# Four-layer graph network on one NeuronCore: own rows added later, mask conversions spread over a stage, buffers and stores of two projections rearranged

## The chip, the cores and the metric

The kernel runs on one core of a Trainium2 chip. A core has a TensorE (PE) for matrix products, a VectorE (DVE), a ScalarE (ACT) and a GpSimd (POOL) for elementwise work, and a SyncE (SP) that only issues transfers; PE, DVE, ACT and POOL each execute their own instructions in order, and semaphores make one engine wait for another. Transfers (DMA) are issued from the queues of SP, ACT and POOL. The metric is the device time of one execution in microseconds, less being better. Matrix products read from on-chip buffers and leave their sums in PSUM, from where DVE or ACT takes them.

## The reference, cut to what matters

The input x has 2708 rows of 512 numbers, adj is a 2708 x 2708 matrix of 0 and 1. Four layers follow one another, each as x = layernorm(x + layer(x)):

```python
# layer 0: mean over the first 64 neighbours of each row, and the row itself
keep = Ab & (cumsum(Ab, axis=1) <= 64)
xj = leaky_relu((keep @ X) / max(cnt, 1) @ W_nb.T + b_nb)
out0 = leaky_relu(X @ W_line.T + b_line) + where(cnt > 0, xj, 0)
# layer 1: mean over all neighbours
self_f = x @ W_self + b_self
nb_f = (mask @ x / max(deg, 1)) @ W_nb + b_nb
out1 = relu(concat([self_f, nb_f]) @ W_comb + b_comb)
# layer 2: attention over the neighbours with 8 heads of 64 columns
# layer 3: attention with 8 heads, elu, attention with one head of 512 columns, elu, then
out3 = relu(h @ lin1_w + lin1_b) @ lin2_w + lin2_b      # 512 -> 1024 -> 512
```

## The kernel before, in words

The 2708 rows are worked on as NT = 22 tiles of P = 128 rows; the last tile has 20 rows. The whole mask stays on the chip, turned, in an 8-bit buffer maskT (one slab of 2816 columns for each tile). Rows of a layer's result go to DRAM and are fetched again where they are needed (fetched(), lines 162 to 165, issued by SP into a buffer called "rows" of the pool "ahead", which has three of them). A tile framework orders each engine's instructions and inserts the waits; `tc.issue_after(x)` puts an instruction behind another on its engine, and `pe` (lines 95 to 101) chains PE's instructions in the order written. Generators (todo, both) hand out small pieces of other work between the products of a loop.

Layer 0's products (loop from line 297 on). For each tile: the product with W_nb (product(), lines 226 to 229, four matmuls of 128x512), split into a high part on ACT and a low part yL on DVE (line 223); for 14 of the mask's tiles also a count on ACT (line 246) and the keep rule on DVE, in two halves, each a running sum (line 252) and a multiplication (line 255), and the turning of the mask by PE; then the product with W_line, the bias (line 317), leaky (line 186) and the addition of the tile's own rows x (line 319). The result u goes to r0_dram. The pair of lines 317 to 319 stands between the two halves of the keep rule on DVE. b_line is fetched on ACT's queue by bias() (lines 214 to 217).

Layer 0's aggregation (loop from line 450 on). Tiles are taken in blocks of four, with sums in PSUM; for each of 22 slabs ACT converts a piece of the mask (kT, line 335) and PE multiplies it with the high and the low part (line 460). Between these products come: the remaining masks (other_masks), the weights of layer 1 (weights1: W_self, W_nb and both halves of W_comb are fetched on SP's queue, some of them through "rows"), the attention vectors (vectors), and finish() for the block before (lines 376 to 386): it fetches r0, adds b_nb, applies leaky, adds r0, normalises, and stores x1. b_nb is another bias(), fetched when this stage begins, into the same single buffer as b_line.

Layer 1's first stage (loop from line 481 on). For each tile: product with W_nb (split as above), the conversion of one slab of the mask from a sign to 0 and 1 on DVE (line 485, 128x2816 eight-bit numbers), then the product with W_self, whose result goes to z1_dram. Its second stage (loop from line 495 on) multiplies the converted mask with the split rows (line 506); ACT widens eight slabs at a time (line 503).

Projections p2, p3 and p4 (project(), from line 566). For each tile: source() gives the rows, PE turns them, multiplies with the weights (line 627), and DVE and ACT make from the product the scaled rows R2 (line 656), and the columns ucol, ecol and vcol. keep_v() (lines 597 to 608) turns the last of them by PE, applies exp on ACT (line 605), collects the columns of a whole block of tiles in vrow, and stores each block at its end on SP's queue. In p3 source is summed() (lines 929 to 938): it fetches o of the attention before (into "rows") and x2 (into "spare", two buffers), multiplies (line 934), adds (line 935), normalises in place with the last step on ACT (line 118), and stores the rows as x3; the same buffer is then turned by PE. p4 takes its rows from elu_turned() and has no summed().

Attention (lines 703, 730, 895 and 799) and the last attention (line 1056) follow. The tiles' MLP is mlp() (lines 1007 to 1039): products with lin1 (line 1022), relu on ACT (line 1024), then for each tile eight products with lin2 (line 1031), the sum with x3, normalisation and the store to out. For the last pair, tiles 20 (128 rows) and 21 (20 rows), nothing else is left to run beside it.

A second, general program (from line 1106 on) is kept for inputs whose values leave the range that the first assumes; it isn't executed in these runs, and the change doesn't touch it.

Of the kernel before, what the change touches and what calls it, by code (L numbers as in the profile page):

```python
# [30 lines left out]
def kernel(  # L31
# [57 lines left out]

    o_dram = dram.tile([N, D], F32, name="o_dram")  # L90
    oT_dram, rc_dram = [], []

    behind = []

# [90 lines left out]
    def leaky(dst, u):  # L185
        return nc.vector.scalar_tensor_tensor(dst, u, 0.01, u, op0=OP.mult, op1=OP.max)
# [7 lines left out]
    with ExitStack() as phase:  # L194
# [16 lines left out]
        sums = lambda dtype=F32, shape=(P, D): ps_a.tile(list(shape), dtype, name="acc", tag="acc")  # L211
        sm = phase.enter_context(tc.tile_pool(name="l01", bufs=2))

        def bias(src):
            b = sm.tile([P, D], F32, name="bias", bufs=1)
            nc.scalar.dma_start(b, src)
            return b

        highs = {}
# [4 lines left out]

        def product(xT, n, w, which, order=as_it_comes):
            pm = ps_mm.tile([P, D], F32, name=f"pm{which}")
            for k in range(KD):
                order(nc.tensor.matmul(pm[:n], xT[:, k, :n], w[:, k, :], start=(k == 0), stop=(k == KD - 1)))  # L228
            return pm
# [45 lines left out]
        with ExitStack() as ph:  # L275
# [21 lines left out]
            for t in range(NT):  # L297
                n = rows(t)
                if t > 1:
                    lows[t] = keep_y(t, n, product(xTs(t, order=pe), n, wnT, 0, pe))  # L300
                xT = xTs(t)
                if t + 1 < NT:
                    xTs(t + 1, order=pe)
                while turned < counted - (t + 1 < NT):
                    for _ in turn(turned, masks(turned), lambda: sums(BF16, (P, G, P)), pe):
                        pass
                    turned += 1
                now = counted < min(HERE, -(-(t - 1) * HERE // (NT - 5)))
                if now:
                    m, places = masks(counted), st.tile([P, N // 2], BF16, name="places", bufs=1)  # L310
                    with tc.issue_after(highs[t].ins):
                        count(counted, m)
                    with tc.issue_after(lows[t].ins):
                        place(counted, m, places, 0, 2)
                pm = product(xT, n, wlT, 1, pe)
                u = sm.tile([P, D], F32, name="u")
                nc.vector.tensor_add(u[:n], pm[:n], b_line[:n])  # L317
                leaky(u[:n], u[:n])
                low = nc.vector.tensor_add(u[:n], u[:n], xs(t))
# [7 lines left out]

        with ExitStack() as ph:
            st = ph.enter_context(tc.tile_pool(name="l0b", bufs=1))
            b_nb = bias(bcast(l0_b_nb, D))  # L330

            def kept(b, j):
                w = (b[1] - b[0]) * P
# [42 lines left out]
            def finish(ts_, us):  # L376
                for t in ts_:
                    n, u = rows(t), us[t]
                    r0 = fetched(r0_dram, t, n)
                    nc.vector.tensor_add(u[:n], u[:n], b_nb[:n])  # L380
                    leaky(u[:n], u[:n])
                    yield
                    nc.vector.scalar_tensor_tensor(u[:n], u[:n], has[:n, t:t + 1], r0, op0=OP.mult, op1=OP.add)
# [156 lines left out]
        nc.vector.tensor_reduce(pick_c[:, g], rows_c, AX.X, OP.add)  # L540


    LAST, TWIN, few = NT - 1, 32, rows(NT - 1)
    assert few <= TWIN
# [21 lines left out]
    def project(name, source, layer, v_dram, cuts, turned=None, first=None):  # L566
# [12 lines left out]
        with ExitStack() as ph:  # L579
# [7 lines left out]
            width = max(z - a for a, z in cuts) * P  # L587
# [7 lines left out]
            vrows, bs, scaled = {}, {}, {}  # L595
# [344 lines left out]
    loads, ready = [], {}  # L940

# [30 lines left out]
    class Last:  # L972
# [34 lines left out]
        def mlp(self, t0, t1, h):  # L1007
# [11 lines left out]
            for f in range(KF):  # L1019
# [4 lines left out]
                nc.scalar.activation(gT[:, f, :w], pl[:, :w], AF.Relu, bias=self.b1[:, f:f + 1])  # L1024
                if f % 2:
                    yield
            for t in range(t0, t1):
                n = rows(t)
                pl = self.ps_l.tile([P, 512], F32, name="pl")
                for f in range(KF):  # L1030
                    nc.tensor.matmul(pl[:n], gT[:, f, (t - t0) * P:(t - t0) * P + n], self.lin2[:, f, :],  # L1031
                                     start=(f == 0), stop=(f == KF - 1))
                    if f == KF // 2 - 1:
                        yield
                y = (self.pool or sm).tile([P, D], F32, name="xT")
                nc.vector.tensor_add(y[:n], pl[:n], x3s[t])
                layer_norm(sm, y[:n], n, y[:n])
                (nc.sync if t1 == NT else nc.gpsimd).dma_start(out[t * P:t * P + n, :], y[:n])
                yield

    quads = [(t, min(t + 4, NT)) for t in range(0, NT, 4)]
# [385 lines left out]
```

## Time and profile before

| what | us |
|---|---|
| median of 3 runs | 2994.57 (2991.03 to 2997.17) |
| profiled execution | 2990.11 |
| its span | 2988.3 |
| PE busy | 2887.4 (97%) |
| DVE busy | 1997.9 (67%) |
| ACT busy | 1533.7 (51%) |
| POOL busy | 219.8 (7%) |

Stages of the profiled execution, by the start of their first matmul or last step, in us from the span's start:

| stage | from | to |
|---|---|---|
| layer 0: products | 0 | 221 |
| layer 0: aggregation, with the weights of layer 1 | 221 | about 500 |
| layer 1: products, then aggregation | about 500, 665 | 885 |
| p2, attention of layer 2 | 886, 977 | 1528 |
| p3, attention of layer 3 | 1528, 1640 | 2190 |
| p4, last attention and MLP | 2190, 2268 | 2988 |

The page gives busy times by engine and groups of equal instructions. A group's line reads: source line, engine, operation, out<-in by the program's names, shapes, the count; then busy time and the mean of one in ns; then the idle time of the engine just before and what ended it. A timeline line reads: start, length, engine, line, operation, and in brackets the idle time before it with the releaser. Since an engine executes in order, a long wait on one engine is only worth its length if the engine that sets the stage's end stands too.

### The profile page before, as it was taken

To read this page: it belongs to the slowest core of one execution; us is meant where nothing else is said; L and a number is where in the kernel's file an instruction comes from. 1 tells how busy PE (TensorE), PEld (TensorE's weight loads), DVE (VectorE), ACT (ScalarE), POOL (GpSimd) and SP (SyncE) were. 2 spreads that over 40 slices of the span, in tenths; PEclk is the share of its full clock that TensorE was granted. 3 is DMA by queue.
4 is the path that set the end of the run, shared out by engine and by line. 5 is a ranking of instruction groups with operands and counts; after the bars stand their busy time and mean duration, and the time that the engine had idled before them with its cause. 6 is when DMAs were issued, how large, how long until landed. Compare 5 with 4: busy or idle time off the path is not lost.

```text
span 2988.3 us, 36484 instructions
## 1 busy us (share of the span) xinstructions
PE 2887.4 (97%) x14456; PEld 1606.4 (54%) x14456; DVE 1997.9 (67%) x2405; ACT 1533.7 (51%) x1774; POOL 219.8 (7%) x341
## 2 busy tenths in 40 slices
PE   8899999999999999999998999999999999999998
PEld 4447766448888333444466333444475555555555
DVE  6976639413234999999976999999964535445242
ACT  3546533113224999999965899999951000000001
POOL 1110101201110000000022000000000000000000
PEclk9999999999999999999999999999999999999999
DMA  4532325312222011111144111111061000000000
GB/s 120 113 92 59 86 72 143 129 62 85 84 74 80 28 52 39 38 48 44 33 126 140 40 40 39 41 55 46 28 160 60 4 25 14 25 14 15 14 22 20
DMA packets 117426, 180.05 MB, mean 60 GB/s; under 512 B 41042, under 2 KB 65507, under 8 KB 117246
## 3 DMA queue, kind: packets, MB, share of 16 engines
q1 hardware_dynamic: 88974, 116.47, 13.3%
q0 software_dynamic: 18160, 57.39, 6.8%
q10 hardware_dynamic: 10112, 3.77, 0.5%
q8 instruction: 116, 1.90, 0.3%
q14 instruction: 64, 0.52, 0.1%
HBM read 147.55 MB, written 44.65 MB: 64 GB/s over the span
## 4 chain that ended last, share of the span: by engine, by line
PE 64%; DVE 21%; ACT 7%; issue 5%; DMA 3%; POOL 0%; SPq 0%; DVEq 0%; POOLq 0%; ACTq 0%
PE pn L1056 13%; PE po L895 13%; DVE e L703 12%; PE acc L506 7%; PE pm L228 7%; PE pm L627 5%; PE pl L1031 5%; PE pl L1022 5%; ACT c L730 4%; PE acc L460 4%; DVE places L252 2%; PE pd L799 2%; PE ps_tr L124 1%; DMA rows<-o_dram 1%; DVE maskT L485 1%
## 5 line engine op out<-in xcount | busy, mean ns | idle before, releaser
L703 DVE SCALAR_TENSOR_TENSOR e<-v_bc,ucol,maskT 128x1408 f32<-128x1408 f32 (+3 forms) x804 | 1135.6, 1469 | 324.4 <-PE pn L1056 314.3
L730 ACT ACTIVATE c<-e,bcol 128x1300 fp8e4<-128x1300 f32 (+1 forms) x688 | 967.7, 1423 | 75.0 <-DVE e L703 30.0
L895 PE MATMUL po<-e,R 128*64 128x512 f32 (+2 forms) x4224 | 903.8, 547 | 30.2 <-DVE e L703 27.2
L895 PEld LDWEIGHTS po<-e,R 128*64 128x64 f32 x4224 | 338.7, 136 | 562.3 <-issue 396.6
L1056 PE MATMUL pn<-e,R 128*128 128x512 f32 (+1 forms) x1056 | 413.4, 542 | 0.0
L1056 PEld LDWEIGHTS pn<-e,R 128*128 128x128 f32 x1056 | 191.0, 190 | 199.3 <-issue 196.1
L1024 ACT ACTIVATE w<-pl,b 128x256 f32<-128x256 f32 (+1 forms) x88 | 40.9, 465 | 372.9 <-PE pl L1022 364.8
L460 PE MATMUL acc<-yH,kT 128*128 128x512 f32 x484 | 197.3, 408 | 5.0 <-ACT kT L335 5.0
L228 PE MATMUL pm<-w,xT 128*128 128x512 f32 (+1 forms) x384 | 177.7, 606 | 22.1 <-DVE yL L223 18.7
L460 PE MATMUL acc<-yL,kT 128*128 128x512 f32 x484 | 189.3, 391 | 0.0
L506 PE MATMUL acc<-yH,mf 128*128 128x512 f32 x484 | 188.4, 389 | 0.0
L506 PE MATMUL acc<-yL,mf 128*128 128x512 f32 x484 | 188.3, 389 | 0.0
L627 PE MATMUL pm<-w,xT 128*128 128x264 f32 (+1 forms) x704 | 171.1, 398 | 3.6 <-DVE R L656 2.2
L228 PE MATMUL pm<-weight,xT 128*128 128x512 f32 (+1 forms) x352 | 160.2, 598 | 2.3 <-DVE u L317 1.5
L1031 PE MATMUL pl<-lin,w 128*128 128x512 f32 (+1 forms) x352 | 157.4, 592 | 0.0
L1022 PE MATMUL pl<-lin 128*128 128x256 f32 (+1 forms) x704 | 153.4, 371 | 3.7 <-DVE lin L924 3.7
L627 PEld LDWEIGHTS pm<-w,xT 128*128 128x128 f32 (+1 forms) x704 | 131.9, 193 | 30.3 <-ACT xT L126 3.0
L1022 PEld LDWEIGHTS pl<-lin 128*128 128x128 f32 x704 | 129.1, 190 | 34.4 <-issue 15.8
L503 ACT CAST mf<-maskT 128x1024 fp32r<-128x1024 fp8e4 (+1 forms) x66 | 64.4, 977 | 158.0 <-PE acc L506 147.9
L222 ACT CAST yH<-pm 128x512 fp32r<-128x512 f32 (+1 forms) x44 | 25.7, 585 | 229.3 <-PE pm L228 229.3
L335 ACT ACTIVATE kT<-maskT 128x512 fp32r<-128x512 fp8e4 (+1 forms) x132 | 77.5, 594 | 116.6 <-PE acc L460 116.6
L228 PEld LDWEIGHTS pm<-w,xT 128*128 128x128 f32 (+1 forms) x384 | 70.8, 189 | 120.4 <-issue 99.2
(215 smaller groups left out, 2713.1 us busy)
## 6 DMA issues: line engine op xcount, KB each, us to landing
rows<-x_dram SPq DMA_DIRECT2D x63, 256.0 KB
v_bc<-v_dram SPq DMA_DIRECT2D x16, 704.0 KB
x_dram<-u POOLq DMA_DIRECT2D x42, 256.0 KB, 2.4
v_bc<-v_dram SPq DMA_DIRECT2D x16, 650.0 KB
m<-in_adj_dram POOLq DMA_DIRECT2D x13, 677.0 KB, 8.5
rows<-in_x_dram SPq DMA_DIRECT2D x21, 256.0 KB
r_dram<-u POOLq DMA_DIRECT2D x21, 256.0 KB, 3.3
rows<-r_dram SPq DMA_DIRECT2D x21, 256.0 KB
```

Source lines behind the costliest of these rows:

```text
L228: order(nc.tensor.matmul(pm[:n], xT[:, k, :n], w[:, k, :], start=(k == 0), stop=(k == KD - 1)))
L335: made = nc.scalar.activation(kT[:, :w], maskT[:, j, b[0] * P:b[0] * P + w], AF.Relu, scale=-1.0)
L460: nc.tensor.matmul(pa[t], kT[:, (t - b[0]) * P:(t - b[0] + 1) * P], y[:, j, :], start=(j == 0 and y is yH), stop=(j == NT - 1 and y is yL))
L503: nc.scalar.copy(mf[:, :g1 - g0, :], maskT[:, g0:g1, t * P:(t + 1) * P])
L506: nc.tensor.matmul(pa, mf[:, j - g0, :], y[:, j, :], start=(j == 0 and y is yH), stop=(j == NT - 1 and y is yL))
L627: nc.tensor.matmul(pm[a][:m, :D // 2 + heads], xT[:, k, :m], w[:, k, a, :D // 2 + heads], start=(k == 0), stop=(k == KD - 1))
L703: self.made = nc.vector.scalar_tensor_tensor(e[:, :w], v[:, :w], ucol[:, j, h:h + 1], maskT[:, j, c0:c0 + w], op0=OP.max, op1=OP.mult)
L730: nc.scalar.activation(c[:, :w], e[:, :w], AF.Sigmoid, bias=bcol[:, j, h:h + 1], scale=STEP, saturate=False)
L895: pe(nc.tensor.matmul(po[i][HO * k:HO * k + HO, :c1 - c0], R2[:, j, h * HO:(h + 1) * HO], e[:, c0:c1], start=(i_ == 0), stop=(i_ == NT - 1)))
L1022: nc.tensor.matmul(pl[:, :w], self.lin1[:, k, f * P:(f + 1) * P], h[:, k, :w], start=(k == 0), stop=(k == KD - 1))
L1031: nc.tensor.matmul(pl[:n], gT[:, f, (t - t0) * P:(t - t0) * P + n], self.lin2[:, f, :], start=(f == 0), stop=(f == KF - 1))
L1056: nc.tensor.matmul(pn[k][:, :w], R2[:, j, k * P:(k + 1) * P], e[:, :w], start=(j == 0), stop=(j == NT - 1))
```

## The change

Eight edits, in the order of the program:

- A constant groups4 is added, which sums four groups of 32 partitions in one matmul.
- bias() takes the queue as an argument; b_nb is fetched on SP's queue, b_line stays on ACT's.
- product() has another path for the last tile where it is not chained by `pe` (layer 1's two products of that tile): the four matmuls go to four groups of 32 PSUM partitions, ACT copies the result, and one matmul with groups4 sums the groups. POOL zeroes the unused columns of xT.
- The addition of the own rows leaves the product loop of layer 0; finish() fetches x beside r0 and adds it to r0 on DVE, behind the last leaky of the product loop.
- The mask conversions of layer 1 are put behind line 223 of the loop's tile t, three tiles late, two each in the last three tiles.
- keep_v() stores each tile's 128 columns by itself, from a buffer of its own (two of them), on ACT's queue.
- summed() fetches o into a pool "o" with three buffers from tile 2 on; the normalised rows x3 go to "rows", and the store and the turning read that.
- In mlp() the last pair takes its tile of 20 rows first, as eight matmuls in four groups of 32 PSUM partitions; ACT copies them, and the sum with groups4 and the tile's end are put into the middle of the other tile's products.

```diff
+    groups4 = const.tile([P, 32], F32, name="groups4")
+    nc.vector.tensor_reduce(groups4, ident.rearrange("p (g n) -> p n g", g=4), AX.X, OP.add)
...
-        def bias(src):
+        def bias(src, queue=nc.scalar):
             b = sm.tile([P, D], F32, name="bias", bufs=1)
-            nc.scalar.dma_start(b, src)
+            queue.dma_start(b, src)
...
         def product(xT, n, w, which, order=as_it_comes):
             pm = ps_mm.tile([P, D], F32, name=f"pm{which}")
+            if n == few and order is as_it_comes:
+                nc.gpsimd.memset(xT[:, :, n:32], 0.0)
+                for k in range(KD):
+                    nc.tensor.matmul(pm[32 * k:32 * k + 32], xT[:, k, :32], w[:, k, :], start=True, stop=True)
+                u = sm.tile([P, D], F32, name="u")
+                nc.scalar.copy(u, pm)
+                pm = sums()
+                nc.tensor.matmul(pm[:few], groups4[:, :few], u, start=True, stop=True)
+                return pm
...
-                leaky(u[:n], u[:n])
-                low = nc.vector.tensor_add(u[:n], u[:n], xs(t))
+                low = rows_made = leaky(u[:n], u[:n])
...
-            b_nb = bias(bcast(l0_b_nb, D))
+            b_nb = bias(bcast(l0_b_nb, D), nc.sync)
...
-                    r0 = fetched(r0_dram, t, n)
+                    r0, x0 = fetched(r0_dram, t, n), fetched(x, t, n)
                     nc.vector.tensor_add(u[:n], u[:n], b_nb[:n])
                     leaky(u[:n], u[:n])
+                    with tc.issue_after(rows_made.ins):
+                        nc.vector.tensor_add(r0, r0, x0)
...
-                keep_y(t, n, product(xT, n, wnb[0], 0))
-                nc.vector.tensor_scalar(maskT[:, t, :], maskT[:, t, :], 0.0, None, op0=OP.not_equal, saturate=False)
+                low = keep_y(t, n, product(xT, n, wnb[0], 0))
+
+                for p in {19: (16, 17), 20: (18, 19), 21: (20, 21)}.get(t, (t - 3,)):
+                    if p >= 0:
+                        with tc.issue_after(low.ins):
+                            nc.vector.tensor_scalar(maskT[:, p, :], maskT[:, p, :], 0.0, None, op0=OP.not_equal,
+                                                    saturate=False)
...
-                a, z = next(c for c in cuts if c[0] <= t < c[1])
-                if t == a:
-                    vrows[a] = sm.tile([heads, width], F32, name="vrow", bufs=1)
-                vrow = vrows[a]
+                vrow = sm.tile([heads, P], F32, name="vrow")
...
-                nc.scalar.activation(vrow[:, (t - a) * P:(t - a) * P + n], ps[:heads, :n], AF.Exp, scale=ALPHA - 1.0)
-                if t == z - 1:
-                    cols = slice(a * P, a * P + (z - 1 - a) * P + n)
-                    nc.sync.dma_start(v_dram[:, cols], vrow[:, :cols.stop - cols.start])
+                nc.scalar.activation(vrow[:, :n], ps[:heads, :n], AF.Exp, scale=ALPHA - 1.0)
+                nc.scalar.dma_start(v_dram[:, t * P:t * P + n], vrow[:, :n])
...
-        o, x2 = fetched(o_dram, t, n), fetched(x2_dram, t, n, late, "spare", 2)
+        o = fetched(o_dram, t, n) if t < 2 else fetched(o_dram, t, n, sm, "o", 3)
+        x2 = fetched(x2_dram, t, n, late, "spare", 2)
...
-        layer_norm(late, o, n, o, on_scalar=True)
-        nc.gpsimd.dma_start(x3_dram[t * P:t * P + n, :], o)
-        return o
+        x3 = o if t < 2 else ahead.tile([P, D], F32, name="rows", bufs=3)[:n]
+        layer_norm(late, o, n, x3, on_scalar=True)
+        nc.gpsimd.dma_start(x3_dram[t * P:t * P + n, :], x3)
+        return x3
...
-            for t in range(t0, t1):
+            held = None
+            for t in sorted(range(t0, t1), key=rows):
                 n = rows(t)
                 pl = self.ps_l.tile([P, 512], F32, name="pl")
+                if n == few and self.pool:
+                    nc.gpsimd.memset(gT[:, :, w:w - n + 32], 0.0)
+                    for f in range(KF):
+                        g = 32 * (f % 4)
+                        nc.tensor.matmul(pl[g:g + 32], gT[:, f, (t - t0) * P:(t - t0) * P + 32], self.lin2[:, f, :],
+                                         start=(f < 4), stop=(f >= KF - 4))
+                    held = t, n, self.pool.tile([P, D], F32, name="xT")
+                    nc.scalar.copy(held[2], pl)
+                    continue
                 for f in range(KF):
                     nc.tensor.matmul(pl[:n], gT[:, f, (t - t0) * P:(t - t0) * P + n], self.lin2[:, f, :],
                                      start=(f == 0), stop=(f == KF - 1))
                     if f == KF // 2 - 1:
+                        if held:
+                            got = self.ps_l.tile([P, 512], F32, name="pl")
+                            nc.tensor.matmul(got[:few], groups4[:, :few], held[2], start=True, stop=True)
+                            end(*held[:2], got)
                         yield
```

More of the change, by code (lines that the diff above doesn't have):

```diff
@@ L91 @@
     oT_dram, rc_dram = [], []
+    few = N - (NT - 1) * P
+    groups4 = const.tile([P, 32], F32, name="groups4")
+    nc.vector.tensor_reduce(groups4, ident.rearrange("p (g n) -> p n g", g=4), AX.X, OP.add)
+    assert few <= 32
     behind = []
@@ L540 @@
         nc.vector.tensor_reduce(pick_c[:, g], rows_c, AX.X, OP.add)
-    LAST, TWIN, few = NT - 1, 32, rows(NT - 1)
-    assert few <= TWIN
+    LAST, TWIN = NT - 1, 32
     nc.sync.dma_start(maskT[TWIN:TWIN + few, LAST, :N], maskT[:few, LAST, :N])
@@ L586, in project @@
                 ps_v, ps_mm = ps_mm, ps_v
-            width = max(z - a for a, z in cuts) * P
             xs = early(1, NT, lambda t: source(sm, t, rows(t)))
@@ L594, in project @@
                 xTs = lambda t: parts(t if t < 3 else (t - 3) // 2 + 3)[:, :, ((t - 3) % 2 if t > 2 else 0) * P:][:, :, :P]
-            vrows, bs, scaled = {}, {}, {}
+            bs, scaled = {}, {}
             def keep_v(t):
                 n = rows(t)
-                a, z = next(c for c in cuts if c[0] <= t < c[1])
-                if t == a:
-                    vrows[a] = sm.tile([heads, width], F32, name="vrow", bufs=1)
-                vrow = vrows[a]
+                vrow = sm.tile([heads, P], F32, name="vrow")
                 ps = ps_v.tile([P, P], F32, name="ps_v")
                 nc.tensor.transpose(ps[:heads, :n], bs[t][:n, :heads], ident[:n, :n])
-                nc.scalar.activation(vrow[:, (t - a) * P:(t - a) * P + n], ps[:heads, :n], AF.Exp, scale=ALPHA - 1.0)
-                if t == z - 1:
-                    cols = slice(a * P, a * P + (z - 1 - a) * P + n)
-                    nc.sync.dma_start(v_dram[:, cols], vrow[:, :cols.stop - cols.start])
+                nc.scalar.activation(vrow[:, :n], ps[:heads, :n], AF.Exp, scale=ALPHA - 1.0)
+                nc.scalar.dma_start(v_dram[:, t * P:t * P + n], vrow[:, :n])
             for t in range(NT):
@@ L1026, in mlp, with end @@
                     yield
-            for t in range(t0, t1):
+            def end(t, n, pl):
+                y = (self.pool or sm).tile([P, D], F32, name="xT")
+                nc.vector.tensor_add(y[:n], pl[:n], x3s[t])
+                layer_norm(sm, y[:n], n, y[:n])
+                (nc.sync if t1 == NT else nc.gpsimd).dma_start(out[t * P:t * P + n, :], y[:n])
+            held = None
+            for t in sorted(range(t0, t1), key=rows):
                 n = rows(t)
                 pl = self.ps_l.tile([P, 512], F32, name="pl")
+                if n == few and self.pool:
[7 more added lines that the diff above has]
+                    continue
                 for f in range(KF):
@@ L1033, in mlp @@
                     if f == KF // 2 - 1:
+                        if held:
+                            got = self.ps_l.tile([P, 512], F32, name="pl")
+                            nc.tensor.matmul(got[:few], groups4[:, :few], held[2], start=True, stop=True)
+                            end(*held[:2], got)
                         yield
[L1035 to L1038, printed above, removed]
+                end(t, n, pl)
                 yield
```

## The prediction

> **What bounds the kernel now.** I began with the page's chain of work that ended last, then the busy times by stage, then, where a stage touched by the change leaves the TensorE (PE) idle, the timeline of the engine that PE waits for. The chain by engine:
>
> ```profile
> PE 64%; DVE 21%; ACT 7%; issue 5%; DMA 3%; POOL 0%; SPq 0%; DVEq 0%; POOLq 0%; ACTq 0%
> ```
>
> The VectorE's (DVE) 21% is mostly line 703 in the two attention stages, which the change leaves alone. So I looked at the stages around them (columns: length, then busy time of PE, PEld, DVE, ACT, POOL, then granted clock, DMA share, GB/s):
>
> ```profile
> 0.00:212.00 212.00, 185.25 (x742) 93.13 (x742) 164.39 (x164) 93.03 (x125) 27.36 (x44) 0.99 0.46 107
> 212.00:528.00 316.00, 307.45 (x1356) 219.21 (x1356) 195.29 (x291) 145.46 (x231) 38.67 (x51) 0.99 0.36 93
> 885.00:977.00 92.00, 90.48 (x459) 74.86 (x457) 37.35 (x125) 42.88 (x122) 9.47 (x32) 1.00 0.28 83
> 1540.00:1636.00 96.00, 86.28 (x397) 68.15 (x396) 67.27 (x205) 50.18 (x126) 30.25 (x59) 0.95 0.49 154
> ```
>
> These are layer 0's products, layer 0's aggregation, layer 2's projection p2 and layer 3's p3. Two leave PE idle: the first (27 us) and p3 (10 us, and fewer matmuls in more time than p2, which does the same PE work). In the first, the timeline of PE:
>
> ```profile
> 118.34 3.67 PE L228 MATMUL pm<-w,xT 128*128 128x512 f32 x8 [1.27 <-DVE yL L223]
> ...
> 123.71 3.70 PE L228 MATMUL pm<-weight,xT 128*128 128x512 f32 x8
> 128.68 3.67 PE L228 MATMUL pm<-w,xT 128*128 128x512 f32 x8 [1.27 <-DVE yL L223]
> ```
>
> and of DVE:
>
> ```profile
> 124.31 0.69 DVE L319 TENSOR_TENSOR u<-u,rows 128x512 f32<-128x512 f32 x1
> 124.92 3.03 DVE L252 TENSOR_TENSOR_SCAN places<-m,places,over 128x1354 bf16<-128x1354 bf16 x1
> 127.87 0.66 DVE L223 TENSOR_TENSOR yL<-pm,yH 128x512 fp32r<-128x512 f32 x1
> ...
> 134.65 0.69 DVE L319 TENSOR_TENSOR u<-u,rows 128x512 f32<-128x512 f32 x1
> ```
>
> One tile takes 134.65 - 124.31 = 10.34 us; DVE works through it without a pause, and PE stands 1.27 us of it, so PE needs 9.07. In p3, SyncE's (SP) timeline of fetches, which come in twos:
>
> ```profile
> 1553.90 4.69 SPq L164 DMA_DIRECT2D rows<-o_dram  x2
> ...
> 1563.47 3.78 SPq L164 DMA_DIRECT2D rows<-o_dram  x2
> ...
> 1573.45 3.70 SPq L164 DMA_DIRECT2D rows<-o_dram  x2
> ...
> 1583.34 0.32 SPq L164 DMA_DIRECT2D rows<-o_dram  x1
> ...
> 1591.90 7.58 SPq L164 DMA_DIRECT2D rows<-o_dram  x2
> ```
>
> Two tiles per 9.9 us, 4.95 each, against 4.11 in p2; from 1590 on it is worse.
>
> **What the Trainium skill says.** "Perfetto Trace Analysis", Identifying Performance Opportunities: the same gap repeating on an engine that should be full can mean too few buffers for the next tile. p3 agrees: the fetch into "rows" (3 buffers) waits until the tile before it was normalised, stored (3.9 us, chain of waits at 1599.05) and transposed. "TensorE: Matmul & The Clock Gate", Measured speedup vs the span model: three products in separate groups of 32 columns ran 2.38 times as fast as one by one. The trace has four such groups at line 799:
>
> ```profile
> 1309.70 1.47 PE L799 MATMUL pd<-c,parts_c 128*12 128x384 fp8e4 x32
> 2960.30 14.00 PE L1031 MATMUL pl<-lin,w 128*128 128x512 f32 x32
> ```
>
> The 32 matmuls stream 24x384 + 8x148 = 10,400 columns in 1.47 us. Line 506's matmuls of 512 columns start 0.23 us apart (665.05, 665.28), so 10,400 columns one after another would take about 4.7 us: a factor of 3 in this trace. (Line 1031 is fp32, 0.43 us per instruction of 512 columns, 16 per tile.) "DMA: Bandwidth & Descriptors", Issuing engines are not separate DMA queues: another issuing engine saves only sequencer time. So I give the stores moved to ScalarE (ACT) and the bias moved to SP no gain in transfer. That agrees: both engines' issues take 0.2 to 0.45 us here, landings some 3 us.
>
> **The change, part by part** (times against the profiled execution, 2990.11 us with a span of 2988.3).
>
> 1. *Addition of own rows out of the product loop.* Line 319 takes 0.69 us and is on the chain of waits 14 times in the stage. The loop stays DVE-bound: 10.34 - 0.69 = 9.65 against PE's 9.07. So -14 x 0.69 = -9.7. In the new DVE order the second mask product (0.78 us) stands ahead of the subtraction of line 223 that PE waits for; where the chain goes through line 223 to PE and not on along DVE (3 tiles without a scan behind), that costs +0.78 each, +2.3. Sum **-7.4**; ends: -9.7 and -4.
>
> 2. *The additions and 22 more fetches in layer 0's aggregation.* 22 x 0.69 = 15 us more on DVE, which is free 121 of 316 us: hidden, and 15 us if that cover were gone. The fetches (256 KB each) take two of three "rows" buffers per tile; on SP, ten weight fetches stand behind them, each behind one that waits for DVE. PE now waits there for one of them:
>
> ```profile
> 394.02 0.69 DVE u L383
> ...
> 395.17 5.67 DMA w<-in_L_gnn_W_comb_dram
> ...
> 400.97 4.44 PE pm L228 x6
> ```
>
> That stall is 1.95 us; in SP's new order W_comb's other half is issued ahead of it, and a pair of row fetches too, so it can come earlier or later by a tile's turn. I take **-1**, ends -3 and +15 (all of the 15 exposed, or four fetches at their landing of 3.9). The second bias goes to SP behind the first two row fetches; its first reader follows a whole aggregation block later (some 50 us): 0. On ACT it was issued at 221.5, and the first conversion for PE did not wait for it: 0.
>
> 3. *Mask conversions spread.* Line 485 is 22 x 1.62 = 35.5 us of DVE, all between 454 and 550. PE's waits there are 2.0 us for line 223 and 0.7 for ACT. Spread behind line 223 of each tile, one conversion per 7.3 us tile of PE work is hidden (DVE is busy 45 of 136 us from 528 on); the last three tiles carry two each, 3.2 us, and are read by ACT only after PE has begun the next stage's first 16 masks. **-2**, ends -2.7 and +2.
>
> 4. *Layer 1's last tile packed* (both products of 20 rows, each 3.4 us at 657.74 and 661.19). Now 3.4/3 = 1.1, then ACT's copy (0.6), then a fold of 0.86 (two fp32 instructions of 0.43): 2.6 each if nothing overlaps, so **-1**; ends -3 and +3 (no concurrency, and a zeroing on POOL waits for the first product).
>
> 5. *v stored per tile on ACT* (3 projections, 22 stores of some 0.4 us issue). ACT is busy 43 of 92 us in p2 and 37 of 78 in p4. **+0.5**; ends 0 and +4. The two ACT table loads that the new order drops (1.28 us each in the trace) were beside DVE-bound work: 0.
>
> 6. *p3's buffers.* o now has its own three, freed when ACT has written the normalised tile; no store and no transpose is in the loop. From the new order of DVE, where the product and sum of tile k+1 stand ahead of the last steps of tile k, the loop is: fetch 3.9 (landing), product 0.69, sum 0.69, variance steps 0.19 + 0.17 + 0.69, PE's R products 0.7, mean 0.17, ACT 0.9: 8.1 us per two tiles, 4.05 each, level with PE's 4.11. p3 takes 112.4 us from the first product (1528.07) to the first attention product (1640.46), p2 91.4. If all came back, -21; two loops this close don't run at the better one's pace, and the early tiles miss a prefetch during attention (+1). I take 4.5 per tile over 22 tiles: 112.4 - 22 x 4.5 = 13.4, **-13**; ends -20 and -5.
>
> 7. *Last tile of the MLP.* Before: 13.86 us for two tiles at line 1031, 6.93 each although one has 20 rows. After: 6.93/3 = 2.3, plus 6.93, plus a fold of 0.86 = 10.1: -3.8; the last store is then 256 KB rather than 40, +0.5. **-3.3**; ends +1.4 (groups one after another) and -4.3.
>
> Sum: -7.4 - 1 - 2 - 1 + 0.5 - 13 - 3.3 = **-27.2**, of which I take -26, since parts 2 and 3 have more room above than below: 2964. The median of the runs shown is 4.46 above the profiled execution, so 2964 + 4.5 = **2968.5**. Within 0.2% (6 us, about what a measurement of this kernel can tell from no change) would be 2988.6 to 3000.6.
>
> **Rivals.** (a) *p3 keeps its pace*: the fetches' latency and DVE's fixed order, not the buffers, hold it at some 4.75 per tile, -8 at most; for it, DVE is busy 67 of 96 us there; against it, the stage's fetches start only on release. With parts 4 and 7 at half: -19, about 2976. (b) *Everything comes back*: p3 at p2's pace, the W_comb stall gone: -36, about 2958. (c) *Slower: SP's queue blocks layer 0's aggregation.* Each of ten weight fetches waits behind a row fetch that itself waits for a buffer held by two fetches per tile; PE executes in order and stands for the landing (3.9 for rows). All ten at 3.9 is +39: 2990 - 26 + 39 + 4.5 = 3007. It decides from 3.3 us per fetch on (10 x 3.3 = the gain of 26 plus 6). Against it: the profile shows PE waiting for only two of them now, and a step of the loop leaves several us between fetch and use. (d) *Packing does nothing*: the fp32 groups run one after another, parts 4 and 7 give +4 instead of -4 (the folds and copies are then pure cost): about 2977.
>
> **Chances.** Forecast 0.5, (a) 0.2, (d) 0.08, (b) 0.12, (c) in full or in part 0.1, of which 0.04 ends within 0.2%. Faster by over 0.2%: 0.9; within: 0.04; slower: 0.06. The range 2955 to 2984 takes in (a), (b) and (d), and part 2's upper end of +15.
>
> **What would show it.** Right: the period of 10.34 becomes about 9.65 with PE waiting some 0.6 per tile; p3's fetches of o come every 4 to 4.5 us and its 112.4 us becomes about 99; line 485's rows are spread to 660; the last two tiles' matmuls take 10 us. Wrong: waits of PE for "rows" or weights between 221 and 528, p3 above 105 us, or a gap of PE in layer 1's first stage behind a conversion.

## The result, and the profile after

| | kernel before | changed kernel |
|---|---|---|
| median | 2995.87 us (4 runs, 2991.03 to 2998.87) | 2971.95 us (4 runs, 2968.18 to 2975.79) |
| ratio, 95% interval | | 0.9925 (0.9912 to 0.9937) |
| profiled execution | 2990.11 us, span 2988.3 | 2975.79 us, span 2973.9 |

The changed kernel is 23.9 us faster by the medians, 22.5 by the ratio; a later run of the same kernel gave 2969.37 against 2993.27, again 23.9 by the medians (ratio 0.9922, 0.9906 to 0.9939). The two profiled executions lie only 14.3 us apart, since before's lies below all four of its runs and after's is the highest of its own. So a comparison of the two traces stage by stage is needed before any sum is believed. The page's own chain of waits after is no help: it was followed back only over the last instructions. The stage table of the changed kernel, by the same marks as before (columns as in the prediction), shows layer 0's products, p2, p3 and the last stage:

```profile
0.00:217.75 217.75, 196.60 (x781) 97.13 (x781) 153.20 (x148) 96.24 (x132) 29.33 (x47) 0.99 0.46 109
...
879.70:975.69 95.99, 90.15 (x454) 74.74 (x454) 37.59 (x126) 47.05 (x126) 8.95 (x30) 0.99 0.29 87
...
1526.16:1627.09 100.93, 94.39 (x458) 75.75 (x459) 74.96 (x236) 58.17 (x145) 30.77 (x65) 0.99 0.54 175
...
2256.63:2973.90 717.27, 700.40 (x2128) 386.93 (x2128) 304.34 (x486) 60.72 (x126) 53.74 (x65) 0.99 0.06 18
```

Against before (220.72, 91.39, 112.39 and 720.44) that is -3.0, **+4.6**, -11.5 and -3.2. Two of these are surprises: the product loop gave 3 and not 7, and p2 got longer.

In the product loop, the timeline of PE:

```profile
129.69 3.67 PE L244 MATMUL pm<-w,xT 128*128 128x512 f32 x8 [0.49 <-DVE yL L230]
139.24 3.67 PE L244 MATMUL pm<-w,xT 128*128 128x512 f32 x8 [0.49 <-DVE yL L230]
```

The period is 139.24 - 129.69 = 9.55 us instead of 10.34, and PE waits 0.49 of it: as forecast. The loop isn't what fell short. The loss lies ahead of it, in the first products of the program, of which this is the first, before and after:

```profile
11.38 3.70 PE L228 MATMUL pm<-w,xT 128*128 128x512 f32 x8 [0.68 <-ACT xT L126]
...
12.00 6.21 PE L244 MATMUL pm<-w,xT 128*128 128x512 f32 x8 [0.68 <-ACT xT L133]
```

The same eight matmuls took 6.21 us. Where that comes from is a question for the runs below.

In p2 the extra time is one wait. PE before and after:

```profile
976.97 8.67 PE L895 MATMUL po<-e,R 128*64 128x512 f32 x40 [0.31 <-ACT vrow L605]
...
975.69 9.75 PE L910 MATMUL po<-e,R 128*64 128x512 f32 x36 [4.78 <-ACT vrow L622]
```

The end of p2 on ACT, before:

```profile
974.49 1.28 ACT L605 ACT_TABLE_LOAD   x1
...
976.58 0.33 ACT L605 ACTIVATE vrow<-ps_v 8x128 f32<-8x128 f32 x2
976.93 1.28 ACT L730 ACT_TABLE_LOAD   x1
978.23 1.47 ACT L730 ACTIVATE c<-e,bcol 128x1408 fp8e4<-128x1408 f32 x1
```

and after:

```profile
971.23 1.28 ACT L745 ACT_TABLE_LOAD   x1
972.52 1.47 ACT L745 ACTIVATE c<-e,bcol 128x1408 fp8e4<-128x1408 f32 x1
974.01 1.28 ACT L655 ACT_TABLE_LOAD   x1
975.30 0.16 ACT L655 ACTIVATE ecol<-pm 20x4 f32<-20x4 f32 x1
975.37 0.20 ACT L657 ACTIVATE ucol<-pm 20x4 f32<-20x4 f32 x2
975.48 0.16 ACT L622 ACTIVATE vrow<-ps_v 8x20 f32<-8x20 f32 x1
```

The last exp of v (line 622) reads a PSUM tile whose room the attention's first products (line 910) take over. Before, ACT did that exp ahead of the sigmoid c (line 730); now the sigmoid (line 745) and the two table loads around it stand ahead of it, 4.0 us.

In p3, SP's fetches of o no longer come in twos, and come faster (3.6 us apart in these lines) than PE uses them (4.1 us per tile where it doesn't wait):

```profile
1553.99 0.32 SPq L171 DMA_DIRECT2D o<-o_dram  x1
...
1557.22 0.32 SPq L171 DMA_DIRECT2D o<-o_dram  x1
...
1560.81 0.32 SPq L171 DMA_DIRECT2D o<-o_dram  x1
...
1564.80 0.32 SPq L171 DMA_DIRECT2D o<-o_dram  x1
```

But not all of p3's gain is a shorter wait. The line of this stage before is

```profile
1528.07:1640.46 112.39, 100.93 (x459) 78.99 (x459) 75.45 (x232) 60.08 (x147) 33.60 (x65) 0.94 0.49 153
```

PE stood idle for 112.39 - 100.93 = 11.5 us of it, after for 6.5, so 5.0 us are waits. The other 6.5 are PE's busy time, 94.39 instead of 100.93 for the same work, with a granted clock of 0.99 instead of 0.94.

And the two packings, layer 1's last tile and the MLP's last pair:

```profile
653.41 1.07 PE L237 MATMUL pm<-w,xT 128*32 128x512 f32 x8
654.82 1.43 PE L237 MATMUL pm<-weight,xT 128*32 128x512 f32 x8 [0.34 <-POOL xT L235]
655.70 1.02 PE L241 MATMUL acc<-u,groups 128*20 128x512 f32 x2
657.86 1.03 PE L241 MATMUL acc<-u,groups 128*20 128x512 f32 x2 [1.14 <-ACT u L239]
```

```profile
2949.67 1.92 PE L1059 MATMUL pl<-lin,w 128*32 128x512 f32 x16
2951.52 3.70 PE L1065 MATMUL pl<-lin,w 128*128 128x512 f32 x8
2955.15 1.04 PE L1070 MATMUL pl<-xT,groups 128*20 128x512 f32 x2
2956.12 3.70 PE L1065 MATMUL pl<-lin,w 128*128 128x512 f32 x8
```

Sixteen instructions of 512 fp32 columns take 2951.52 - 2949.67 = 1.85 us in groups of 32, where the same sixteen as a whole tile took 6.93: a factor of 3.7, more than the 3 of the forecast. The pair takes 10.1 us in place of 13.86.

### The profile page after: what moved, and what is told of

Read it like the earlier page. It is cut to its first block, busy times and chain, and to the rows that moved or that the text cites. A ratio compares the mean times of both kernels' runs of the same rounds, so it can differ in the third digit from the quotient of the medians.

```text
span 2973.9 us, 36611 instructions
## 1 busy us (share of the span) xinstructions
PE 2879.2 (97%) x14462; PEld 1605.8 (54%) x14462; DVE 1998.3 (67%) x2406; ACT 1536.7 (52%) x1775; POOL 207.9 (7%) x344
## 5 line engine op out<-in xcount | busy, mean ns | idle before, releaser
L120 POOL TENSOR_TENSOR ln_rs<-ln_rs,half 128x1 f32<-128x1 f32 (+1 forms) x88 | 54.2, 616 | 1449.3 <-DVE ln_rs L119 1380.8
L1065 PE MATMUL pl<-lin,w 128*128 128x512 f32 x336 | 150.8, 593 | 0.0
L642 PEld LDWEIGHTS pm<-w,xT 128*128 128x128 f32 (+1 forms) x704 | 128.7, 188 | 30.2 <-ACT xT L133 4.5
```

The source lines that it names most:

```text
L642: nc.tensor.matmul(pm[a][:m, :D // 2 + heads], xT[:, k, :m], w[:, k, a, :D // 2 + heads], start=(k == 0), stop=(k == KD - 1))
```

## The experiments

All stages by their first matmuls, in us, from each kernel's own profiled execution. "Third" is the start of the third tile's first product, "loop" from there to the end of layer 0's products, "to L1b" from there to layer 1's second stage. The attention stages (549 to 552 and 544 to 547) and layer 1's second stage (220.9) are left out, since they don't differ by kernel. The medians come from four occasions, on which the kernel before had 2995.87, 2992.57, 2994.56 and 2993.27; each ratio below is against the kernel before of the same occasion.

| kernel | median | third | loop | to L1b | p2 | p3 | p4 | last |
|---|---|---|---|---|---|---|---|---|
| before | 2995.87 | 32.1 | 188.6 | 444.0 | 91.4 | 112.4 | 83.3 | 720.2 |
| before_again | 2999.79 (1 run) | 37.1 | 188.6 | 444.7 | 91.4 | 115.1 | 82.9 | 720.7 |
| groups_only | 2994.88 (1 run) | 34.5 | 188.2 | 443.1 | 91.4 | 113.5 | 83.3 | 720.9 |
| rows_only | 2988.16 | 37.1 | 181.2 | 443.3 | 91.4 | 114.0 | 83.5 | 720.9 |
| v_only | 2996.18 | 34.1 | 188.6 | 443.7 | 96.0 | 106.2 | 83.7 | 720.6 |
| v_block_act | 2990.05 | 32.1 | 188.6 | 444.2 | 91.4 | 108.4 | 83.1 | 720.7 |
| p3_and_v | 2985.32 | 35.6 | 188.6 | 442.4 | 96.0 | 100.4 | 83.7 | 720.2 |
| after | 2971.95 | 37.0 | 180.8 | 441.1 | 96.0 | 100.9 | 84.2 | 717.0 |
| after_again | 2969.37 | 34.4 | 180.8 | 438.9 | 96.0 | 100.4 | 83.4 | 716.5 |
| after_nospread | 2972.42 | 36.4 | 180.8 | 441.6 | 96.0 | 98.8 | 84.7 | 716.8 |
| after_nopack | 2974.42 | 36.9 | 180.8 | 441.4 | 96.0 | 105.5 | 84.6 | 720.7 |
| after_o2 | 2980.66 | 34.2 | 180.8 | 439.2 | 96.0 | 111.6 | 84.5 | 717.2 |
| after_vfirst | 2965.56 | 37.7 | 180.8 | 439.8 | 90.9 | 98.2 | 84.9 | 716.5 |
| after_best | 2963.81 | 34.6 | 180.8 | 439.1 | 90.9 | 97.2 | 83.2 | 717.0 |

"Loop" and p2 repeat to 0.4 us and the last stage to 0.7 among kernels that are alike there. p3 doesn't: it takes 112.4 to 115.1 in the four kernels without the parts that bear on it, and 97.2 to 105.5 in the seven with the store by tiles and three buffers for o. "Third" scatters by 5.6. What p3 consists of in each trace (idle is its length less PE's busy time):

| kernels | p3 | PE busy | PE idle | granted clock |
|---|---|---|---|---|
| before, before_again, groups_only, rows_only | 112.4 to 115.1 | 97.9 to 100.9 | 11.5 to 16.3 | 0.94 to 0.97 |
| v_block_act | 108.4 | 93.7 | 14.7 | 1.00 |
| v_only | 106.2 | 96.9 | 9.3 | 0.97 |
| p3_and_v, after, after_again, after_nospread | 98.8 to 100.9 | 92.8 to 94.4 | 5.9 to 7.1 | 0.99 to 1.00 |
| after_nopack | 105.5 | 97.1 | 8.4 | 0.95 |
| after_o2 | 111.6 | 98.4 | 13.2 | 0.97 |
| after_vfirst, after_best | 97.2 to 98.2 | 92.7 to 93.0 | 4.5 to 5.1 | 1.00 |

**rows_only**: before, with the addition moved.

```diff
-                low = nc.vector.tensor_add(u[:n], u[:n], xs(t))
+                low = rows_made = leaky(u[:n], u[:n])
...
-                    r0 = fetched(r0_dram, t, n)
+                    r0, x0 = fetched(r0_dram, t, n), fetched(x, t, n)
...
+                    with tc.issue_after(rows_made.ins):
+                        nc.vector.tensor_add(r0, r0, x0)
```

> The kernel before with one part alone: the own rows are added in the aggregation instead of the product loop (bias and all else as before). My theory: a tile of layer 0's product loop takes 9.56 us instead of 10.34, the loop gives 7 to 8 us between its third tile and its end, the aggregation keeps its length within 1 us; total 7 to 8 us less than before. Rival 1: the 22 extra fetches on SyncE's queue hold up weight fetches in the aggregation, which grows by 3 us or more, total within 4 us of before. Rival 2 on the 4.8 us that the changed kernel lost before its third tile: if they come from the new constant's reduction on the VectorE, they can't appear here; if they are a lower TensorE clock of single executions, they appear in some profiles and not in others, whatever the kernel.

Measured: ratio 0.9976 (0.9965 to 0.9987), so some 7 us less (4.4 by the medians). The loop gives 7.4 (188.6 to 181.2), the stretch behind it keeps its length (443.3), and rival 1 falls. The late start (37.1) is here without the constant, so the constant isn't needed for it.

**v_only**: before, with v stored by tiles.

```diff
+                vrow = sm.tile([heads, P], F32, name="vrow")
...
-                if t == z - 1:
-                    nc.sync.dma_start(v_dram[:, cols], vrow[:, :cols.stop - cols.start])
+                nc.scalar.dma_start(v_dram[:, t * P:t * P + n], vrow[:, :n])
```

> The kernel before with one part alone: v stored tile by tile on the ScalarE's queue. My theory: in the ScalarE's order one sigmoid between two table loads (1.28 + 1.47 + 1.28 us) now stands ahead of the last exp of p2 that frees TensorE's banks, so p2 takes 96 us instead of 91.4 and p4 0.5 to 1 us more; p3 keeps its 112; total 4 to 6 us more than before. Rival: the 4.8 us wait in p2 belonged to that one execution of the changed kernel; then p2 takes 91 to 92 here and the total stays within 2 us.

Measured: ratio 1.0008 (1.0000 to 1.0016). p2 takes 96.0, as the theory said, in this and every kernel with this store and the scheduler's own order: the wait is the order's, not chance. But the theory missed p3: 106.2, some 7 less than the 112.4 to 115.1 of the four kernels that store blocks on SP's queue; PE's idle time there fell from some 15 to 9.3. So the total was hardly slower. This trace flatters the kernel, though: its execution took 2992.01, 4 us under the median. By the ratio the whole is 2.4 us longer (0 to 4.8), and p2 and p4 account for some 5 of that, which leaves p3 a gain of about 3 and not 7.

**after_nospread**: the changed kernel with line 485's conversion back where it was.

```diff
-                low = keep_y(t, n, product(xT, n, wnb[0], 0))
-                for p in {19: (16, 17), 20: (18, 19), 21: (20, 21)}.get(t, (t - 3,)):
...
+                keep_y(t, n, product(xT, n, wnb[0], 0))
+                nc.vector.tensor_scalar(maskT[:, t, :], maskT[:, t, :], 0.0, None, op0=OP.not_equal, saturate=False)
```

> The changed kernel with the mask conversions of layer 1 put back as before (one per tile, not tied to the subtraction, not late). My theory: the VectorE is the late one only at the entry of layer 1, so 2 to 3 us come back as waits of TensorE for the subtraction; total 2 to 3 us more than the changed kernel. Rival: now that the VectorE also adds the own rows there, the pile of conversions costs more, 5 us or above.

Measured: ratio 0.9929 (0.9916 to 0.9942) beside the changed kernel's 0.9925 and 0.9922, so 1 to 2 us, within the intervals' width. In its trace PE waits 2.3 us for the subtraction (line 230) in layer 1's first stage, against 1.5 in the changed kernel's and 0.6 in after_vfirst's; "to L1b" is 441.6 against a mean of 439.6 over the five kernels with spread and packing (438.9 to 441.1). The size agrees with the theory, but single executions scatter by as much, so that a gain from the spread isn't shown; nor is there a sign of the rival's 5 us.

**after_vfirst**: the changed kernel with the ScalarE's order held.

```diff
-            keep_v(NT - 1)
+            kept = keep_v(NT - 1)
+            if first:
+                first.__self__.behind = kept
...
+            with tc.issue_after(self.behind.ins):
+                nc.scalar.activation(c[:, :w], e[:, :w], AF.Sigmoid, bias=bcol[:, j, h:h + 1], scale=STEP, saturate=False)
```

> The changed kernel with one order added on the ScalarE: every sigmoid of the attention (c) stands behind the last exp of v of its projection. My theory: p2 loses the 4.8 us wait and several table loads, taking 90 to 91.5 us instead of 96; p3 loses up to 1.5 us; the attentions keep their length, since the c's are needed only by the divisors, later; total 4 to 6 us less than the changed kernel. Rival: the c's that come later hold up the divisors, so that the attention stage of layer 2 grows by what p2 gives.

Measured: ratio 0.9904 (0.9892 to 0.9917), 2965.56 us. p2 takes 90.9, 5.1 less, and the attention behind it keeps its length (550.9). PE, then ACT at the end of p2:

```profile
970.13 6.23 PE L914 MATMUL po<-e,R 128*64 128x512 f32 x30 [0.86 <-ACT vrow L622]
```

```profile
969.90 0.18 ACT L622 ACTIVATE vrow<-ps_v 8x20 f32<-8x20 f32 x1
970.22 1.28 ACT L749 ACT_TABLE_LOAD   x1
971.52 1.47 ACT L749 ACTIVATE c<-e,bcol 128x1408 fp8e4<-128x1408 f32 x1
```

The table load and the sigmoid now come behind the exp. The cause of p2's loss is shown: the order on ACT, not the store itself.

**v_block_act**: before, with the block's store on ACT's queue.

```diff
-                    nc.sync.dma_start(v_dram[:, cols], vrow[:, :cols.stop - cols.start])
+                    nc.scalar.dma_start(v_dram[:, cols], vrow[:, :cols.stop - cols.start])
```

> The kernel before with v stored by whole blocks as before, but on the ScalarE's queue. It tells apart why the store tile by tile shortens p3's second half. Theory A: the block's store stood in SyncE's queue and held up the fetches of rows behind it; then p3 takes 105 to 108 us here. Theory B: what counts is the place of the two wide v loads, which here stand one fetch of rows earlier in SyncE's queue than with the store tile by tile, ahead of two fetches that then share the DMA engines with them; then p3 stays at 111 to 114. In both, p2 stays at 91 to 92, since the ScalarE's order has the last exp ahead of the sigmoid.

Measured: ratio 0.9991 (0.9983 to 0.9999), p2 91.4, p3 108.4. So ACT's queue alone costs p2 nothing; the 4.6 us come only with the store tile by tile. p3 lies between the theories, but neither has an effect of that size in the trace. PE stands idle in this p3 as long (14.7) as in the kernels with the store on SP's queue (11.5 to 16.3); what is shorter is its busy time, 93.7, at a granted clock of 1.00. For theory A, the store before stood between two fetches of o, and here they follow one another:

```profile
1583.34 0.32 SPq L164 DMA_DIRECT2D rows<-o_dram  x1
1587.01 0.29 SPq L608 DMA_DIRECT2D v_dram<-vrow  x1
1587.39 0.32 SPq L164 DMA_DIRECT2D rows<-o_dram  x1
...
1582.20 3.79 SPq L164 DMA_DIRECT2D rows<-o_dram  x2
```

From the first issue to the end of the second it is 4.37 us before and 3.79 here: the store held up the fetch by 0.6 us, not by 5. For theory B, the two fetches of o behind the wide v loads are issued 7.5 us apart here, 7.3 in before and 7.2 in v_only, so their place made no difference to that gap. Why p3 is shorter with the store off SP's queue stays open. This trace, too, comes from the fastest of its 13 executions (2986.22, median 2990.05); by the ratio the whole gains 2.7 us (0.3 to 5.1).

**p3_and_v**: before with two parts, the store by tiles and o's buffers (both edits as in the change).

> The kernel before with two parts: v stored tile by tile on the ScalarE's queue, and o's own buffers in p3. My theory: p3 is then all that the changed kernel's is, 98 to 101 us against 106 with the store alone and 112 to 114 without both, so the buffers are worth 5 to 8 us and the store 6 to 8; p2 has its 96 us; total 7 to 9 us less than before. Rival: the gain in p3 also needs another part of the change; then p3 stays above 103.

Measured: ratio 0.9970 (0.9959 to 0.9981), 9 us less; p3 100.4, p2 96.0. Nothing else of the change is needed for p3. What the buffers give is less clear: by the traces about 6 (106.2 to 100.4), by the ratios of the two kernels 11 (an estimate from 0.9970 and 1.0008, some 7 to 15 with both intervals).

**after_o2**: the changed kernel, two buffers for o.

```diff
-        o = fetched(o_dram, t, n) if t < 2 else fetched(o_dram, t, n, sm, "o", 3)
+        o = fetched(o_dram, t, n) if t < 2 else fetched(o_dram, t, n, sm, "o", 2)
```

> The changed kernel with two buffers for o in p3 instead of three. My theory, that the loop from the normalised tile back to its fetch sets p3's pace: with two buffers the fetch waits for the tile before the last, p3's middle falls from 4.5 us per tile to 5 to 6, and p3 takes 108 to 120 us instead of 99 to 101. Rival: with the store and the turning out of the loop two are enough, the VectorE's order sets the pace; p3 then stays within 2 us.

Measured: ratio 0.9953 (0.9940 to 0.9966), p3 111.6. SP's fetches come in twos again, two tiles per 9.1 us:

```profile
1555.91 3.23 SPq L171 DMA_DIRECT2D o<-o_dram  x2
...
1564.90 3.23 SPq L171 DMA_DIRECT2D o<-o_dram  x2
...
1574.05 3.50 SPq L171 DMA_DIRECT2D o<-o_dram  x2
```

PE waits 14 times, 8.0 us in all, for the normalised rows. The changed kernel's trace has 3 such waits, 1.7 us in all. PE's idle time in p3 is 13.2 against 6.5, and the whole takes 8 to 9 us more than the changed kernel by the ratios. The count of buffers matters: the rival falls.

**after_nopack**: both packings off (the two conditions on `n == few` made false, the last pair in its old order).

> The changed kernel without both packings: the tiles of 20 rows go through as whole tiles again, in layer 1's last products and in the MLP's last pair. My theory: the last stage grows by 3.3 us (716.9 to 720.2) and the stretch of layer 0's aggregation and layer 1's first stage by 1 to 2; total 4 to 5 us more than the changed kernel. Rival: the groups of 32 columns do not run at the same time on fp32 numbers, and what the last stage gained is the end of the smaller tile that moved into the other's products; then the eight packed matmuls take about 7 us in the changed kernel's trace, and this kernel loses under 2 us.

Measured: ratio 0.9935 (0.9922 to 0.9948), 3 to 4 us more than the changed kernel, within the intervals; the last stage is 720.7 again, and "to L1b" 441.4. The eight packed matmuls take 1.85 us in the changed kernel, so the rival falls. (p3's 105.5 here holds one wait of 4.2 us, for line 649, that no other of these kernels shows. The 16 matmuls of the tile behind it took 6.1 us, against 3.8 in a tile before it.)

**before_again** and **groups_only** (before with the constant alone, two lines at its head), one execution each:

> The kernel before once more, for the same. My theory: the third tile's product starts anywhere between 32 and 38 us; p2 91.4 and the last stage 720 repeat, p3 between 111 and 115. Rival: the early start (32.1 us) belongs to the kernel before, and comes again.

> The kernel before with the new constant alone. If the constant's reduction on the VectorE delayed the start, the third tile's product comes after 34 us here; if the first products' pace is a matter of the execution, it lies anywhere between 32 and 38 us, and all other stages are those of before.

Measured: third tile at 37.1 and 34.5 us. The first product of before_again:

```profile
11.80 6.51 PE L228 MATMUL pm<-w,xT 128*128 128x512 f32 x8 [0.67 <-ACT xT L126]
```

Unchanged code now takes 6.51 us where it took 3.70. The late start belongs to the execution, not to the change.

**after_again**:

> The changed kernel once more, for the spread between executions. My theory: the stages repeat within 1 us except p3 (98 to 105) and the first 35 us (third tile's product from 34 to 38 us on), where TensorE's pace in the first products differs by execution. Rival: the late start belongs to the changed kernel: then its third tile starts after 36 us again.

Measured: third tile at 34.4, so the rival falls; p3 100.4, p2 96.0; but p4 took 83.4 and not 84.2.

**after_best**: after_vfirst, with p4's store by blocks on SP's queue.

```diff
+                whole = name == "p4"
+                a, z = next(c for c in cuts if c[0] <= t < c[1]) if whole else (t, t + 1)
...
+                if t == z - 1:
+                    w = (t - a) * P + n
+                    (nc.sync if whole else nc.scalar).dma_start(v_dram[:, a * P:a * P + w], vrow[:, :w])
```

> The changed kernel with the ScalarE's order of after_vfirst and, in p4 alone, v stored again by whole blocks on SyncE's queue. My theory: p2 stays at 91, p3 at 98 to 100, and p4 gives back its 1 us (83.1 to 83.7 instead of 84.2 to 84.9); total 5 to 8 us less than the changed kernel. Rival: p4's extra 1 us isn't the ScalarE's issues but the shorter start of a stage that waits for the attention before; then p4 stays above 84.

Measured: 2963.81 us (2963.64 to 2966.09), ratio 0.9904 (0.9888 to 0.9921), beside after_again's 2968.71 to 2971.19 on the same chip: 5.6 us less, the runs don't overlap. p4 took 83.2; since after_again's took 83.4 with the store by tiles, p4's part in it isn't shown. Of the gain, 5.1 is p2's; p3's 3.2 lies within its scatter.

## Why the prediction was right, and where it was not

The forecast was 2968.5 for a median of 2971.95. Of the 3.4 us between them, 1.3 lie in the kernel before, whose median a fourth run moved from 2994.57 to 2995.87; the gain was 23.9 where 26 had been taken. By its own parts, with the means of the table:

| part | forecast | measured | from |
|---|---|---|---|
| 1 own rows | -7.4 | -7.8 | loop 188.6 to 180.8 |
| 2 fetches in the aggregation | -1 | -0.4, within the scatter | rows_only 443.3 against the mean 443.7 of the six others without spread and packing |
| 3 spread | -2 | about -2, within the scatter | after_nospread |
| 4 layer 1's last tile | -1 | -1.6 | 7.0 to 5.4 us |
| 5 v stored by tiles | +0.5 | +4.6 in p2, up to +0.5 in p4, -7.5 in p3 | v_only's trace |
| 6 o's buffers | -13 | -6 | trace of p3_and_v against v_only's |
| 7 MLP's last pair | -3.3 | -3.8 | last stage 720.6 to 716.8 |

These sum to -24, the measured difference (-7.8 - 0.4 - 2 - 1.6 + 4.6 + 0.5 - 7.5 - 6 - 3.8). With p3's scatter, that they meet it so closely is chance.

Parts 1, 4 and 7 held in mechanism and size; of parts 2 and 3 it is shown only that they are small. In its even stretch the loop stays bound by DVE and gives its 0.69 and a little more; over the whole loop 7.8 us came of 14 x 0.69 = 9.7, near the 7.4 forecast, though the term of +2.3 behind that isn't shown by itself. The W_comb wait fell from 1.95 us to 1.1, and no new one for a fetch came, so rival (c) has no place to stand. (The wait for the aggregation's first masks, 2.1 and 2.6 us in the two traces of before, is 3.4 and 3.1 in those of the changed kernel; the forecast had no term for that.) Rival (d) falls with the factor of 3.7. p3's 100.2 us (mean of the seven kernels with both of its parts, after_o2 apart; 101.2 without after_vfirst and after_best) is 4.55 per tile against the 4.5 taken. Rivals (a) at 4.75 and (b) at 4.11 miss that mean on either side, though after_nopack's one trace has 4.8.

**Part 5 was the step that failed.** It priced the store as "22 stores of some 0.4 us issue" and said of ACT's new order only that the two table loads it drops are worth 0. It named no instruction whose place decides PE's next start. In the new order a sigmoid between two table loads stands ahead of p2's last exp, and PE waits for that exp. That is +4.6 where the upper end given was +4. It also put the store's effect on p3 at nothing, where it gave some 3 us by the ratio and 7 by the trace. The two misses offset each other: v_only's whole, 2.4 us more, lies inside the range of 0 to +4, and that is luck.

**Part 6 had the right total for p3, and its account of it holds only in part.** p3 as a whole came to 113.8 - 100.2 = 13.6 against 13. The forecast took all of it for shorter waits, ended by o's buffers. By the table of p3, some 8 us are waits (PE's idle time, 14.8 to 6.4 on the mean). The other 5 are PE's busy time, at a granted clock that rose with the change; the forecast put that at nothing, although its own line of p3 has a clock of 0.95. In the traces the clock falls to half for 3.4 or 6.8 us at a time, in before at 1606.9, 0.9 us behind the end of the longest wait of its p3 (2.4 us). But v_block_act has waits of 2 to 3 us and keeps 1.00, so what decides isn't shown. Nor is the split between the store and the buffers: 7.6 and 5.8 by the traces, some 3 and 11 by the ratios. The loop of 8.1 us per two tiles isn't the limit that it was taken for: o is fetched every 3.7 us on the mean, not every 4 to 4.5, and over half of what p3 still takes above p2's 91 lies in its first five tiles and its tail.

The page of the Trainium skill that part 5 leaned on, "DMA: Bandwidth & Descriptors", Issuing engines are not separate DMA queues, says that another issuing engine saves only the sequencer's time. No run here speaks against that: the fetch behind the store came 0.6 us sooner. What it cost lay on the engine, in the order of ACT's other instructions, of which that section doesn't speak.

## What to carry to other kernels

When a change puts stores on an engine that also computes, read that engine's new order up to the next instruction that another engine waits for. Here an exp that frees PSUM room for PE came to stand behind a sigmoid and two table loads; one order hint gave back 5.1 us, more than the 4.6 that the new order had cost. Before two traces are subtracted, repeat one of them: the first 35 us and p3 differ by several us between executions of the same kernel, and a trace's own execution can lie 4 us from its kernel's median. And split a stage's time into PE's busy and idle time, with the granted clock beside it: five of p3's 13.6 us weren't waits.

## What the runs showed of the hardware

The first eight fp32 matmuls of the program took 3.70 to 6.77 us over 14 executions of kernels that are alike there. In the slow ones successive matmul instructions start 0.85 us apart at first and 0.43 afterwards, half the pace and then the full one. In the changed kernel's trace the pace turns near 17.1 us, and there its records of the clock begin; ahead of them the clock column reads 1.00 because nothing is recorded. The Trainium skill's page "TensorE: Matmul & The Clock Gate" (What's actually happening) says that the clock gate works on a free-running window, so that the cost of the start differs by run; the spread agrees. Packing four groups of 32 columns gave a factor of 3.7 with fp32; the 2.38 that the same page gives (Measured speedup vs the span model) is for three groups, so the two can't be compared directly.
